# A bias read from PSUM, wider PSUM tiles for layer 0, and one shared region for tanh buffers in a two-layer attention kernel

## The chip, the cores and the metric

The kernel runs on one core of a Trainium2 chip. The metric is the device time of one execution in microseconds (us). A core has a matrix engine (TensorE, PE in the profile, with its weight loads shown apart as PEld), VectorE (DVE), ScalarE (ACT), GpSimd (POOL), and SyncE (SP), which here only issues transfers. PE writes its results to PSUM, eight banks of 512 fp32 columns on 128 partitions; the rest lies in SBUF. Everything is in fp32.

## The reference

The input `x` has 8 batches of 1024 tokens (64 x 16) with 128 features. Layer 0 is an attention of 8 heads followed by a feed-forward block; its softmax is taken twice, once over the 64 positions `m`, once over the 16 positions `g`. Layer 1 has an additive attention, a projection with batch statistics, and a recurrence over the 1024 tokens.

```python
# layer 0, per head
scores = jnp.einsum('bhlfc,bhmgc->bhlfmg', q, k) / jnp.sqrt(jnp.float32(c))
a = jax.nn.softmax(scores, axis=4)
a = jax.nn.softmax(a, axis=5)
z = jnp.einsum('bhlfmg,bhmgc->bhlfc', a, v)
# ... output projection, layer norm, relu(z1 @ w1.T + b1) @ w2.T + b2, layer norm

# layer 1: additive attention
Wi = jnp.einsum('bnd,ed->bne', B, W)
scores = jnp.einsum('d,bijd->bij', v, jnp.tanh(Wi[:, None, :, :] + Wi[:, :, None, :]))
attn = jax.nn.softmax(scores, axis=-1)
# layer 1: recurrence
yt = jax.nn.sigmoid(wx_t + yt @ Vt)
```

The largest part of the work is the tanh: for every pair of tokens i, j of a batch, 128 features. It is symmetric in i and j, so about half of the pairs are computed.

## The kernel before, in words

`fast_path` builds a list of operations with their inputs, outputs, a priority and the engines that may do each, with a cost for each engine. `Plan.emit` (L460) then walks through time: it starts whatever can start first on some engine, and among those nearly ready the one with the lowest priority number. Its order becomes the order in each engine's queue, which the chip keeps. An operation can take a buffer from a set (`Bank`), which a later operation gives back; the planner holds it until then. `port=True` on a VectorE operation tells the planner that it shares a port with GpSimd, so the two aren't planned at once. `ROWS`, `L0` and `L1` are priorities in units of batches: layer 0 of batch b+1 is planned beside layer 1 of batch b.

*Layer 0* (`layer0`, L802), for each head and 128 query tokens: `scores` (L869) are two products of 512 columns into one of two PSUM tiles `sc` of two banks. ACT takes their exponential in place (L872). VectorE sums it (L876) and inverts the sums (L877), and multiplies `sc` by them into `e` in SBUF (L880). For two query tiles together ACT takes the second exponential of `e` (L890), VectorE sums and inverts again (L893, L894), GpSimd multiplies (L904). PE transposes `e` four 128 x 128 blocks at a time (L783) into `m0` or `m1`, PSUM tiles of one bank; VectorE (in batch 0 also ACT) copies each bank to `aT` (L795, L793). `attend` (L918) multiplies with the values into `m0` or `m1`, and `gather` (L925) adds to `zs`. The projections for a head (L833, evicted in L839 or L837; L847, evicted in L795 or L793) and the hidden layer (L965, L971) go through one bank at a time as well. In the first half of batch 0 the two halves of `sa` serve as further banks (`four`). `through_bank` (L773) is the helper: a product into a bank, then an eviction.

*Layer 1* (`layer1`, L1140). For a block `it` of 128 tokens, `group` (L1006) handles 4k tokens i at a time against the tokens j from the block's start (or from the group's own start) on, in one of five SBUF slots `th` of 4 x 1024 columns (three in the first part of batch 0). The 4k rows stand in four parts c, of k rows each; within a group that doesn't begin a block, the row of part c begins at token 4 r0 + c. Either ACT does everything, one instruction for each row with the token's own column as bias (`tanh_row`, L1029); or GpSimd (`add_rows`, L1039) or VectorE write the sums and ACT takes the tanh of all that they filled in as few instructions as possible (`wide_tanh`, L1087). VectorE does a row at a time with k < 4, in a form that also writes an accumulator that nobody reads (`add_row`, L1033), and otherwise `add_rows` with both inputs in SBUF and `port` set. PE then multiplies the rows with `v` into `sa` (`times_v`, L1107), four 32-column products for the four parts side by side, and gives the slot back. When a block's rows are done, ACT takes the exponential of `sa` into `E` (L1203); there are 46 of these. The order of the blocks is set so that narrow and wide blocks share `sa`.

After the plan the recurrence runs (L1398 to L1442), as 32 chunks beside each other, and writes the output.

PSUM before: `sa` (2 banks), `sc0`, `sc1` (2 each), `m0`, `m1` (1 each).

Of the kernel before, what the change touches and what calls it, by code (L numbers as in the profile page):

```python
# [15 lines left out]
P = 128  # L16
# [395 lines left out]


class Plan:
# [45 lines left out]
    def emit(self, slack=0.15, switch=0.1, stay=0.015):  # L460
# [26 lines left out]
        def start_at(n, t, e):  # L487
            take = ops[n][5]
            if take:
                t = max(t, min(bank_free.get(c[0], 0.0) for c in take.of(e)))  # L490
# [23 lines left out]
        while any(open_.values()):  # L514
# [10 lines left out]
            if take:  # L525
                take.name, take.tile = min(take.of(e), key=lambda c: bank_free.get(c[0], 0.0))
                bank_free[take.name] = never
# [11 lines left out]
            if give:  # L539
                bank_free[give.name] = done[n] + self.LATENCY[e]  # L540
# [25 lines left out]
def fast_path(ctx: ExitStack, tc: tile.TileContext, a: dict, fits):  # L566
# [50 lines left out]
    ths = ring("th", 5, [P, 4 * N])  # L617
# [16 lines left out]
    m1 = tile_of(psum, "m1", [P, 512])  # L634
    two = (("m0", m0), ("m1", m1))
    four = two + (("sa0", sa[:, 0:512]), ("sa1", sa[:, 512:1024]))


    def early(k, name, eng):
        t = ths[k // 4][:, (k % 4) * N : (k % 4 + 1) * N].rearrange("p (h c) -> p h c", c=C)  # L640
        eng.dma_start(out=t, in_=a[name])
        return t
# [76 lines left out]
    for h in range(H):  # L719
        nc.tensor.matmul(m1[:, 0:1], wo[:, h, :], bvn[:, h : h + 1], start=h == 0, stop=h == H - 1)  # L720
    nc.vector.scalar_tensor_tensor(zb, m1[:, 0:1], float(M), bo, ALU.mult, ALU.add)
# [51 lines left out]
    def through_bank(pe, weight, r, evict, where, more, w, pri, choice=two):  # L773
# [13 lines left out]
    def copy(dst):  # L787
        def fn(e, bank):
            src = bank
            if len(dst.shape) == 3:  # L790
# [11 lines left out]
    def layer0(b):  # L802
# [16 lines left out]
        for n_part, part in enumerate(parts):  # L819
            qts = range(NT) if part is None else range(4 * part, 4 * part + 4)  # L820

            banks = four if alone and n_part == 0 else two
            for h in range(H):
# [3 lines left out]
                if alone:  # L827
                    vp, kvp = ths[3 + h // 4][:, h % 4 * N : (h % 4 + 1) * N].rearrange("p (t c) -> p t c", c=C), ("vp0", h)
                for s in range(2) if part is None else (part,):
                    cols = slice(s * 512, (s + 1) * 512)  # L830

                    def project(bank, h=h, cols=cols):
                        nc.tensor.matmul(bank, A[:, h, :], xT[:, cols], start=True, stop=True)  # L833

                    def biased(e, bank, h=h, u=u, cols=cols):
                        if e == "ACT":
                            nc.scalar.activation(u[:, cols], bank, AF.Identity, bias=ub[:, h : h + 1])  # L837
                        else:
                            nc.vector.tensor_scalar(u[:, cols], bank, ub[:, h : h + 1], None, ALU.add)  # L839

                    through_bank(project, 0.9, [kx], biased, evict(0.75), [], [("u", h % 2, s)], L0, banks)
                for s in () if alone and n_part else range(2):

                    def values(bank, h=h, s=s):
                        for i in range(4):
                            t = 4 * s + i
                            nc.tensor.matmul(  # L847
                                bank[:, i * P : (i + 1) * P], xT[:, t * P : (t + 1) * P], Wvo[:, h, :], start=True, stop=True
                            )

                    through_bank(
                        values, 0.95, [kx], copy(vp[:, 4 * s : 4 * s + 4, :]), evict(0.68), [], [kvp + (s,)], L0, banks
                    )
                for qt in qts:
                    L0 = pace(n_part, h + (qt - qts[0]) / len(qts))
                    i = (n_part * H + h) * len(qts) + qt - qts[0]
                    sc, kc = scs[i % 2], ("sc", i % 2)
# [4 lines left out]
                    r1, r2 = st[:, q, 0:G], st[:, :, G : G + M]  # L862
                    sc3 = sc.rearrange("p (m g) -> p m g", g=G)
                    e3 = e.rearrange("p (m g) -> p m g", g=G)

                    def scores(_, sc=sc, u=u, qt=qt):
                        for s in range(2):
                            cols = slice(s * 512, (s + 1) * 512)
                            nc.tensor.matmul(sc[:, cols], u[:, qt * P : (qt + 1) * P], xT[:, cols], start=True, stop=True)  # L869

                    add(("PE", 1.74), scores, r=[kx, ("u", h % 2, qt // 4)], w=[kc], pri=L0)
                    add(("ACT", 0.98), lambda _, sc=sc: nc.scalar.activation(sc, sc, AF.Exp, scale=SCALE),  # L872
                        r=[kc], w=[kc], pri=L0)

                    def first_sums(_, sc=sc, r1=r1):
                        nc.vector.tensor_reduce(r1, sc.rearrange("p (m g) -> p g m", g=G), AX.X, ALU.add)  # L876
                        nc.vector.reciprocal(r1, r1)  # L877

                    def divide(_, e3=e3, sc3=sc3, r1=r1):
                        nc.vector.tensor_tensor(e3, sc3, r1.unsqueeze(1).to_broadcast([P, M, G]), ALU.mult)  # L880

                    add(("DVE", 1.49), first_sums, r=[kc], w=[k1], pri=L0)
                    add(("DVE", 1.22), divide, r=[kc, k1], w=[ke], pri=L0)
# [15 lines left out]
                    for q in range(2):  # L899
# [7 lines left out]
                        for s in range(2):  # L907
                            through_bank(
                                transposes([e[:, t * P : (t + 1) * P] for t in range(4 * s, 4 * s + 4)]), 0.52, [ke],
# [600 lines left out]
```

## Time and profile before

| | |
|---|---|
| median of 3 runs | 5395.53 us (5393.81 to 5401.85) |
| the profiled execution | 5395.36 us, of which the span of the profile 5393.6 |
| busy in the span | PE 5044.0, PEld 2771.6, DVE 4933.6, ACT 5099.2, POOL 4496.0 us |
| tanh on ACT | 953 wide (2629 us), 2084 rows (1502 us) |
| sums for tanh | POOL 2268 (3319 us), DVE 1754 rows (1542 us) and 94 others |
| waits for a `th` slot (released by L1107) | POOL 299, DVE 40, ACT 29 us |

A group line of the profile reads: line, engine and operation, output <- inputs (tiles' names without their numbers), shape of output <- input, count; after the bar busy time in us and mean ns of one; after the second bar the engine's idle time just before these instructions and what ended it. A window line gives the length of a stretch and then, for PE, PEld, DVE, ACT and POOL, busy time and count, and at the end the granted TensorE clock and the DMA's share and rate. The ends of matmuls are modelled, so they overlap in the rows.

### The profile page before, as it was taken

The numbers are of one execution on the slowest core, as the hardware profiler recorded it, in microseconds if no ns is written. First come the engines' busy times: TensorE is split into PE (matmuls) and PEld (weight loads), VectorE is DVE, ScalarE is ACT, GpSimd is POOL, SyncE is SP. The second block draws the span as 40 slices with busy tenths as digits, with TensorE's granted clock in tenths as the row PEclk, the third lists the DMA queues.
The fourth block names the chain that finished last, engine by engine and source line by source line (L and its number), as shares of the span: only waits on it lengthen the run. The fifth ranks groups of instructions, "written<-read, shape, count | busy, mean of one in ns | idle before, by whom it ended". The sixth has DMA issues, their size and how long they took to land.

```text
span 5393.6 us, 99434 instructions
## 1 busy us (share of the span) xinstructions
PE 5044.0 (94%) x39173; PEld 2771.6 (51%) x39173; DVE 4933.6 (91%) x8326; ACT 5099.2 (95%) x4190; POOL 4496.0 (83%) x3078
## 2 busy tenths in 40 slices
PE   8999999999999999999999999999999999995566
PEld 6655554555555455555555555545555455542125
DVE  7998989899999999899998999999998999999886
ACT  5489999999999999999999999999999999999994
POOL 2364779798989899899998989898898998996992
PEclk9999999999999999999999999999999999998999
DMA  2000000000000000000000000000000000000001
GB/s 62 1 5 1 1 1 5 1 9 1 1 5 6 4 1 1 5 9 1 1 5 5 5 1 1 5 5 5 1 1 3 7 1 1 1 30 8 1 1 68
DMA packets 27341, 37.73 MB, mean 7 GB/s; under 512 B 2512, under 2 KB 19280, under 8 KB 26864
## 3 DMA queue, kind: packets, MB, share of 16 engines
q1 hardware_dynamic: 24832, 27.99, 1.6%
q8 instruction: 310, 5.08, 0.4%
q10 hardware_dynamic: 1872, 3.16, 0.2%
q14 instruction: 167, 1.37, 0.1%
q0 software_dynamic: 160, 0.13, 0.0%
HBM read 19.22 MB, written 12.06 MB: 6 GB/s over the span
## 4 chain that ended last, share of the span: by engine, by line
PE 56%; ACT 19%; DVE 18%; issue 6%; POOL 1%; DMA 0%; DVEq 0%; ACTq 0%; SPq 0%; POOLq 0%
PE sa L1107 20%; PE m L918 11%; PE sc L869 10%; ACT th L1087 10%; PE m L783 6%; ACT th L1029 5%; DVE th L1033 5%; DVE stat_e L876 2%; DVE stat_e L893 2%; DVE wx L880 2%; ACT sc L872 2%; ACT wx L890 2%; PE m L1236 2%; DVE aT L795 2%; PE m L847 1%
## 5 line engine op out<-in xcount | busy, mean ns | idle before, releaser
L1039 POOL TENSOR_TENSOR th<-wiT 128x1024 f32<-128x1024 f32 (+54 forms) x2268 | 3318.7, 1500 | 318.2 <-PE sa L1107 298.8
L1087 ACT ACTIVATE th<-th 128x4096 f32<-128x4096 f32 (+55 forms) x953 | 2629.0, 2788 | 22.6 <-DVE th L1039 9.5
L1107 PE MATMUL sa<-th,vpat 128*32 128x512 f32 (+33 forms) x24576 | 2037.4, 462 | 235.6 <-ACT th L1087 223.3
L1033 DVE TENSOR_SCALAR_CACHE_REDUCE th<-wiT 128x512 f32<-128x512 f32 (+57 forms) x1754 | 1542.3, 879 | 156.7 <-PE sa L1107 40.3
L1029 ACT ACTIVATE th<-wiT 128x384 f32<-128x384 f32 (+60 forms) x2084 | 1502.5, 792 | 29.2 <-PE sa L1107 28.9
L1107 PEld LDWEIGHTS sa<-th,vpat 128*32 128x32 f32 x24576 | 662.8, 110 | 1372.1 <-issue 844.3
L904 POOL TENSOR_TENSOR wx<-wx,stat_e 128x1024 f32<-128x1024 f32 x512 | 983.9, 1944 | 389.4 <-DVE stat_e L894 320.8
L869 PE MATMUL sc<-xT,wx 128*128 128x512 f32 x2048 | 981.2, 604 | 11.3 <-DVE wx L880 10.7
L918 PE MATMUL m<-aT,wx 128*128 128x256 f32 x3584 | 823.7, 383 | 4.7 <-DVE aT L795 4.5
L918 PEld LDWEIGHTS m<-aT,wx 128*128 128x128 f32 x3584 | 668.1, 190 | 187.5 <-issue 48.0
L880 DVE TENSOR_TENSOR wx<-sc,stat_e 128x1024 f32<-128x1024 f32 x512 | 624.2, 1219 | 25.0
L876 DVE TENSOR_REDUCE stat_e<-sc 128x16 f32<-128x1024 f32 x512 | 619.7, 1210 | 25.8 <-ACT sc L872 25.3
L795 DVE COPY aT<-m 128x512 f32<-128x512 f32 x927 | 600.3, 674 | 36.7 <-PE m L783 34.3
L783 PEld LDWEIGHTS m<-ident,wx 128*128 128x128 f32 x3940 | 443.5, 141 | 326.0 <-issue 156.9
L893 DVE TENSOR_REDUCE stat_e<-wx 128x128 f32<-128x2048 f32 x256 | 583.2, 2278 | 19.1 <-ACT wx L890 18.4
L783 PE MATMUL m<-ident,wx 128*128 128x128 f32 x3940 | 562.6, 278 | 29.7 <-DVE aT L795 14.3
L872 ACT ACTIVATE sc<-sc 128x1024 f32<-128x1024 f32 x512 | 512.7, 1007 | 62.3 <-PE sc L869 56.0
L869 PEld LDWEIGHTS sc<-xT,wx 128*128 128x128 f32 x2048 | 354.7, 190 | 374.4 <-issue 329.3
L890 ACT ACTIVATE wx<-wx 128x2048 f32<-128x2048 f32 x256 | 487.7, 1905 | 30.1 <-DVE wx L880 29.9
L894 DVE RECIPROCAL stat_e<-stat_e 128x128 f32<-128x128 f32 x256 | 243.9, 953 | 8.8
L847 PEld LDWEIGHTS m<-Wvo,xT 128*128 128x128 f32 x1080 | 134.4, 192 | 53.0 <-issue 26.9
L847 PE MATMUL m<-Wvo,xT 128*128 128x128 f32 x1080 | 145.5, 281 | 4.4 <-DVE aT L795 2.4
(183 smaller groups left out, 2887.0 us busy)
## 6 DMA issues: line engine op xcount, KB each, us to landing
xT<-in_xt_dram SPq DMA_DIRECT2D x8, 512.0 KB, 3.6
th<-in_x_dram SPq DMA_DIRECT2D x8, 512.0 KB, 6.8
parked<-X SPq DMA_DIRECT2D x16, 256.0 KB, 2.3
xr<-parked SPq DMA_DIRECT2D x8, 512.0 KB, 8.1
parked_wx<-bT SPq DMA_DIRECT2D x14, 256.0 KB, 2.0
wx<-parked_wx SPq DMA_DIRECT2D x7, 512.0 KB, 4.3
out_dram<-ot ACTq DMA_DIRECT2D x8, 256.0 KB, 2.1
out_dram<-ot SPq DMA_DIRECT2D x8, 256.0 KB, 2.8
```

The source lines that it names most:

```text
L783: nc.tensor.transpose(bank[:, i * P : (i + 1) * P], s, ident)
L795: nc.vector.tensor_copy(dst, src)
L869: nc.tensor.matmul(sc[:, cols], u[:, qt * P : (qt + 1) * P], xT[:, cols], start=True, stop=True)
L876: nc.vector.tensor_reduce(r1, sc.rearrange("p (m g) -> p g m", g=G), AX.X, ALU.add)
L880: nc.vector.tensor_tensor(e3, sc3, r1.unsqueeze(1).to_broadcast([P, M, G]), ALU.mult)
L904: nc.gpsimd.tensor_tensor(e3, e3, r2[:, q, :].unsqueeze(2).to_broadcast([P, M, G]), ALU.mult)
L918: nc.tensor.matmul(bank()[:, :256], vp[:, t, :], aT[:, t, :], start=t == 0, stop=t == NT - 1)
L1029: nc.scalar.activation(rows(c)[:, r, :], wiT[:, i0 + begin[c] :], AF.Tanh, bias=w_i(c, r))
L1033: nc.vector.tensor_scalar(rows(c)[:, r, :], wiT[:, i0 + begin[c] :], w_i(c, r), 0.0, ALU.add, ALU.add, accum_out=unused)
L1039: eng.tensor_tensor(rows(c), wiT[:, i0 + begin[c] :].unsqueeze(1).to_broadcast(shape), w_i(c).unsqueeze(2).to_broadcast(shape), ALU.add,)
L1087: nc.scalar.activation(slot()[:, a:z], slot()[:, a:z], AF.Tanh)
L1107: nc.tensor.matmul(sa[32 * c : 32 * c + 32, s:s1], vpat[:, 31 - r0 - r : 63 - r0 - r], rows(c)[:, r, s - at0 - begin[c] : s1 - at0 - begin ...
```

## The change

Four things change together; the planner then makes a new order.

1. *VectorE's bias.* `m1` goes; its bank is now `near`. For every 64 tokens VectorE copies their columns from `wiT` into a 64-column part of `near` (seven parts in turn). VectorE's additions are all `tensor_tensor` with the bias as first input, from PSUM, over `per` rows at once, and no longer set `port`. The first 64 columns of `near` take the inverted sums of layer 0 (`r1`).
2. *Layer 0 through two-bank tiles.* `sc0` and `sc1` (in the first half of batch 0 also `sa`) now serve scores, all eight transposes of a query tile, the projections and two hidden blocks at a time; single-bank products may use `m0`, `sc0` or `sc1`. The score's exponential goes from PSUM straight to `e`, and the sums and the division work on `e`.
3. *One region.* The five slots become one tile of 20 x 1024 columns. A group takes 4k (w - 4 r0) columns where there is room (`Room`, `Span`), the first part of batch 0 within the first 12 x 1024.
4. *Rectangles.* All rows of a group begin at token 4 r0. A group is filled in pieces of `per` rows, in token order; a group that ACT doesn't do by rows has one wide tanh.

```diff
+class Room:
+    def place(self, n, now, top):
+        best = None
+        for i, (a, _, _) in enumerate(self.spans):
+            t, z = now, a
+            for _, z, free in self.spans[i:]:
+                t = max(t, free)
+                if z - a >= n:
+                    break
+            if z - a >= n and a + n <= top and (best is None or (t, a) < best):
+                best = (t, a)
+        return best
...
-    ths = ring("th", 5, [P, 4 * N])
+    room = 20 * N
+    th = tile_of(work, "th", [P, room])
+    ring_room = Room(th, room)
...
-    m1 = tile_of(psum, "m1", [P, 512])
-    two = (("m0", m0), ("m1", m1))
-    four = two + (("sa0", sa[:, 0:512]), ("sa1", sa[:, 512:1024]))
+    near = tile_of(psum, "near", [P, 512])
+    two = tuple((f"sc{i}", t) for i, t in enumerate(scs))
+    three = two + (("sa", sa),)
+    any_of = (("m0", m0),) + two
...
-            banks = four if alone and n_part == 0 else two
+            wide = three if alone and n_part == 0 else two
+            banks = any_of + wide[2:]
...
-                    add(("PE", 1.74), scores, r=[kx, ("u", h % 2, qt // 4)], w=[kc], pri=L0)
-                    add(("ACT", 0.98), lambda _, sc=sc: nc.scalar.activation(sc, sc, AF.Exp, scale=SCALE),
-                        r=[kc], w=[kc], pri=L0)
+                    through_bank(
+                        scores, 1.74, [kx, ("u", h % 2, qt // 4)],
+                        lambda _, bank, e=e: nc.scalar.activation(e, bank, AF.Exp, scale=SCALE), ("ACT", 0.98), [], [ke], L0, wide,
+                    )
...
+                    def first_sums(_, e=e, s1=s1, r1=r1):
+                        nc.vector.tensor_reduce(s1, e.rearrange("p (m g) -> p g m", g=G), AX.X, ALU.add)
+                        nc.vector.reciprocal(r1, s1)
+
+                    def divide(_, e3=e3, r1=r1):
+                        nc.vector.tensor_tensor(e3, r1.unsqueeze(1).to_broadcast([P, M, G]), e3, ALU.mult)
...
-                        for s in range(2):
-                            through_bank(
-                                transposes([e[:, t * P : (t + 1) * P] for t in range(4 * s, 4 * s + 4)]), 0.52, [ke],
-                                copy(aT[:, 4 * s : 4 * s + 4, q * P : (q + 1) * P]), evict(0.68), [],
-                                [("aT", na, q, s)], L0, banks,
-                            )
+                        through_bank(
+                            transposes([e[:, t * P : (t + 1) * P] for t in range(NT)]), 1.04, [ke],
+                            copy(aT[:, :, q * P : (q + 1) * P]), evict(1.24), [], [("aT", na, q)], L0, wide,
+                        )
...
-        slot = Bank(*slots[: 3 if first_half else 5])
-
-        begin = [0 if r0 == 0 else 4 * r0 + c for c in range(4)]
...
+        slot = Span(ring_room, 4 * k * (w - 4 * r0), 12 * N if first_half else 20 * N)
+        if 4 * r0 % 64 == 0:
+            n = count.setdefault("near", 0)
+            count["near"] = n + 1
+            count["near", it] = n % 7
+            cols, own = near[:, 64 * (n % 7 + 1) : 64 * (n % 7 + 2)], wiT[:, i0 + 4 * r0 : i0 + 4 * r0 + 64]
+            add(("DVE", 0.15), lambda _, cols=cols, own=own: nc.vector.tensor_copy(cols, own), r=all_wi,
+                w=[("near", n % 7)], pri=ROWS - 0.03)
...
+        W = w - 4 * r0
+        per = (1, 1, 1, 2, 2, 4, 8, 16)[it]
+        pieces = 4 * k // per
...
-            nc.vector.tensor_scalar(
-                rows(c)[:, r, :], wiT[:, i0 + begin[c] :], w_i(c, r), 0.0, ALU.add, ALU.add, accum_out=unused
-            )
...
+            if e == "DVE":
+                own = biases[:, 4 * r0 % 64 + p * per : 4 * r0 % 64 + (p + 1) * per].unsqueeze(2).to_broadcast(shape)
+                nc.vector.tensor_tensor(rows(p), own, others, ALU.add)
+            else:
+                own = w_i(p * per, per).unsqueeze(2).to_broadcast(shape)
+                nc.gpsimd.tensor_tensor(rows(p), others, own, ALU.add)
```

In the changed kernel's numbering the lines that the prediction names are: scores L947, their exponential L951, transposes L854, copies L866 and L868, VectorE's additions L1125, GpSimd's L1128, row tanh L1118, wide tanh L1159.

More of the change, by code (lines that the diff above doesn't have):

```diff
@@ L827, in layer0 @@
                 if alone:
[L828 to L841, printed above, removed]
```

232 lines of the change are left out of this document (134 added, 98 removed).

## The prediction

> **What bounds the kernel now.** I read the page's busy lines and slices first, then the stage windows, then the rows of idle time by form. The page has four engines nearly full:
>
> ```profile
> PE 5044.0 (94%) x39173; PEld 2771.6 (51%) x39173; DVE 4933.6 (91%) x8326; ACT 5099.2 (95%) x4190; POOL 4496.0 (83%) x3078
> ...
> ACT  5489999999999999999999999999999999999994
> ```
>
> ACT has two weak slices at the start and one at the end. I cut the span at three of the 46 exponentials that read `sa` (L1203): the 1st at 421 us, the 7th at 994, the 37th at 4748 (about where layer 0 ends). Columns: length, then busy time of PE, PEld, DVE, ACT, POOL.
>
> ```profile
> 0.00:421.00 421.00, 393.31 (x1913) 260.10 (x1914) 363.16 (x486) 274.73 (x420) 181.10 (x116) 1.00 0.08 22
> 421.00:994.00 573.00, 549.40 (x3983) 311.91 (x3985) 523.33 (x783) 547.35 (x600) 440.26 (x289) 0.99 0.01 2
> 994.00:4748.00 3754.00, 3666.08 (x29061) 1998.35 (x29054) 3508.06 (x5847) 3716.94 (x2792) 3409.55 (x2346) 1.00 0.01 4
> 4748.00:5297.00 549.00, 363.25 (x3676) 135.81 (x3674) 482.16 (x1049) 532.13 (x284) 461.65 (x324) 0.94 0.03 9
> ```
>
> Before 421 us PE leads (393 of 421) and ACT idles 146 us. From 421 on ACT is the limit: idle 26, 37 and 17 us in the three later stages. PE is close behind in the long stage, idle 88 of 3754 us. So the sum to make is ACT's work by stage, with PE as the second limit.
>
> **The rows that price the edits.** Columns of a group: form, count, busy us, mean ns of one, idle before.
>
> ```profile
> L880 DVE TENSOR_TENSOR wx<-sc,stat_e 128x1024 f32<-128x1024 f32 x512 | 624.2, 1219 | 25.0
> ...
> L795 DVE COPY aT<-m 128x512 f32<-128x512 f32 x927 | 600.3, 674 | 36.7 <-PE m L783 34.3
> ...
> L1033 DVE DVE_READ_ACCUMULATOR th<-wiT 128x1 f32 x1754 | 144.7, 82 | 0.0
> ...
> L1039 DVE TENSOR_TENSOR th<-wiT 128x1024 f32<-128x1024 f32 x13 | 22.6, 1779 | 0.0
> ...
> L1033 DVE TENSOR_SCALAR_CACHE_REDUCE th<-wiT 128x1024 f32<-128x1024 f32 x7 | 8.9, 1273 | 0.2
> ...
> L872 ACT ACTIVATE sc<-sc 128x1024 f32<-128x1024 f32 x512 | 512.7, 1007 | 62.3 <-PE sc L869 56.0 <-issue 2.5 <-ACT th L1029 1.7
> ...
> L1087 ACT ACTIVATE th<-th 128x4096 f32<-128x4096 f32 x27 | 97.6, 3613 | 0.2 <-DVE th L1039 0.2
> ...
> L1087 ACT ACTIVATE th<-th 128x3072 f32<-128x3072 f32 x12 | 33.0, 2753 | 0.0
> ...
> L1203 ACT ACTIVATE E<-sa 128x1024 f32<-128x1024 f32 x26 | 26.2, 1008 | 0.0
> ```
>
> *VectorE's bias in a PSUM bank.* An addition of 1024 elements now costs 1273 + 82 ns with the accumulator's read. With both inputs in SBUF it took 1779 ns (L1039), with one in PSUM and one in SBUF 1219 ns (L880). The new one (L1125) is of the last kind: 152 ns fixed and 1.042 ns an element. The planner's order, counted in both built programs, has 1754 + 94 VectorE additions before (1.199 million elements a partition) and 1419 after (1.340 million). Before: 1542 us and some 130 for the 94. After: 1419 x 0.152 + 1.340 x 1042 = 1612, and 128 copies of 64 columns into the bank at 0.2 (26). So some 35 us less for 12% more elements. A broadcast that repeats a PSUM word is in no row: it lies between 1219 and 1779 ns for 1024; I take 1219, the row with the same memories. At 1779, 1.34 million elements x 0.55 ns add 733 us.
>
> *Two-bank tiles.* VectorE's 1075 copies of 512 (674 ns, 725 us) become 542 of 1024; 674 is 141 + 533, so one is 1207 and all 654: 71 less. Its 112 biases (82 us) become 67 of mixed width (75). With the additions VectorE loses about 114 us of 4934, which pays only where VectorE was late. ACT's 91 copies of 512 (593 ns, 54 us) become 41 of 1024 (at L872's 1007 ns, 41): 13 less. The exponential of the scores writes `e` in SBUF, not `sc`: L872 in place in PSUM has 1007 ns, L1203 from PSUM to SBUF 1008, so nothing. [...] `first_sums` reads `e` in SBUF: L876 from PSUM has 1210, L893 from SBUF 2278 for twice as much, so the same slope, and nothing.
>
> *The tanh region.* Groups take 4kW columns of 20 x 1024, not one of five slots. The mean group has 4.22 million / 1376 = 3070 columns, so some 6.6 fit for 5. That relieves POOL's 299 us, VectorE's 40 and ACT's 29 of waiting for `sa` (L1107) to free a slot. Of these only ACT's is on the path. Groups become rectangles: 11,300 elements more. ACT's wide tanh goes from 953 (2.962 million) to 1024 (3.137), its single rows from 2084 (1.262 million) to 1708 (1.098). At 0.840 ns an element (3613 - 2753 over 1024) the busy times leave 148 ns fixed for a wide one and 212 for a row. After: 1024 x 0.148 + 3137 x 0.840 = 2787; 1708 x 0.212 + 1098 x 0.840 = 1284. Together 4071 against 4132: 61 less.
>
> PE has the same products and transposes, and 1471 changes between attention rows and other products in place of 1743. A 512-column product takes 521 ns from start to start where the kind changes and 429 where not, so some 25 us come off PE.
>
> **The sum.** ACT: -61 - 13 and -1 for fewer biases against more ReLUs = -73 to -75. By stage, cutting the after program's order at the same three exponentials and pricing both alike (the prices overstate ACT by 3%, scaled to the windows): to the 1st 39 us less, to the 7th 11, to the 37th 15, to the end 4. PE does 52 us less before the 1st exponential (29 of layer 0's pairs of query tiles precede it, not 34) and gets them back before the 37th (+49, -25 for changes).
> - To the 1st: PE led with 93%; at that share it would give 56, ACT's own is 39. I take 39, the lower.
> - To the 7th: 11. PE's idle 24 covers it.
> - To the 37th: 15. PE's idle 88 falls to 88 - 15 - 49 + 25 = 49. It fits, but no more than another 49 could come here.
> - To the end 4; the recurrence (96 us) is untouched.
>
> 39 + 11 + 15 + 4 = 69. The profiled execution has 5395.4 (span 5393.6 and 1.8 around it), which is the median 5395.5 within 0.2. **Forecast 5326 us**, -1.3%.
>
> **Rivals.**
> 1. *The start gains nothing.* `e` is now held from the score's matmul on, since the matmul waits for its place (before, the division by VectorE was the first to need it). Two pairs are in flight. One pair's chain: scores, transposes, scores 1.72 + 0.87 + 1.72, exponential 1.0, sums and division 2.7, second exponential 1.9, sums 3.2, POOL 1.9, transposes 0.87 = 16 us, some 18 with hand-overs. Two in flight give 9 us a pair at best; the trace has 10.9 (16 pairs from 38 to 201 us), and VectorE has 10.5 us of work a pair to queue. At 1 us more for each of 22 pairs and no other gain at the start: 5395 - 30 (the later stages) + 22 = 5387; with the start unchanged 5365. For it: ACT's 56 us behind the score matmuls. Against: scores come right behind the transposes that free `e`, on the same engine.
> 2. *Slower: PE waits for the two-bank tiles.* `sc0` and `sc1` alone carry scores, eight transposes and the projections of layer 0. Before, scores had them to themselves and transposes had two other banks. PE issues in order: behind a blocked transpose stand the attention rows that free `th`, for which POOL, VectorE and ACT wait. It decides from 69 us / 1152 takings (512 scores, 512 transposes, 128 projections) = 0.06 us each; at 0.12 each the time is 5395 - 69 + 138 = 5464, at 0.09 5430. For it: PE in the long stage has 2% left. Against: `sc` is freed by the exponential, no longer by reduction and product, so it is held some 6 us for a score and 4 for a transpose, 20 of the 40 tile-us that two tiles have in a pair's 20 us.
> 3. *More than ACT's work.* The region and the shorter VectorE lines also take half of ACT's 80 us of idling after 421 us, or PE leads the start down to 365: 5326 - 40 = 5286, with both some 5270.
> 4. *The change doesn't free VectorE:* the PSUM broadcast runs like L1039's 1779 ns. VectorE at 4820 + 733 = 5553 becomes the bound, some 5700.
>
> **Chances.** Forecast (5300 to 5350) 48%; less at the start (5350 to 5400) 20%, of which half is faster by over 0.2% (about what a measurement here can tell from no change), 8 points within it and 2 slower; more 15%; slower by the tiles 14%, by the broadcast 3%. Faster 0.48 + 0.15 + 0.10 = 0.73; same 0.08; slower 0.19. The range leaves out the broadcast, half of the tiles' case and the lowest tail: 5275 to 5430.
>
> **What would show it.** ACT's busy time 5020 to 5030 and its rows 1708; VectorE's L1125 at 1.04 ns an element and no POOL addition longer than now; the 1st exponential of `sa` near 380 us and the 37th near 4680; PE's idle before score and transpose products near what L869 and L783 have now (11 and 39 us). If L947 or L854 wait 60 us or more for ACT or VectorE, rival 2 holds; if the 1st exponential stands at 420, rival 1. The forecast is wrong if ACT idles over 70 us more than its 294.

## The result and the profile after

The changed kernel takes 5532.1 us (median of 4 runs) where the kernel before took 5398.7 beside it: a ratio of 1.0253, 95% interval 1.0241 to 1.0266. It is slower by 133 us. The forecast was 5326, and its range ended at 5430. The profiled execution of the changed kernel spans 5530.1 us, 136.5 more than before.

The busy lines and the chain of work of the changed kernel, first of all:

```profile
PE 5046.3 (91%) x39173; PEld 2815.8 (51%) x39173; DVE 5159.8 (93%) x5689; ACT 5045.6 (91%) x3835; POOL 4469.6 (81%) x2711
...
DVE 55%; PE 26%; ACT 10%; issue 8%; POOL 1%; DMA 0%; DVEq 0%; SPq 0%; ACTq 0%; POOLq 0%
DVE stat_e L955 14%; DVE th L1125 12%; PE sa L1179 9%; DVE stat_e L972 7%; DVE wx L959 7%; ACT th L1159 6%; DVE aT L868 6%; PE sc L947 4%; PE m L995 3%; PE sc L995 3%; PE sc L854 2%; DVE stat_e L973 2%; DVE near L956 2%; ACT th L1118 2%; DVE wx L868 1%
```

ACT does 54 us less than before, as was wanted, and yet idles 484 us instead of 294. VectorE, which should have lost 114 us, does 226 more, and the chain now runs through it for 55% of the span (18% before). The largest single line of the chain is L955, the first sums. The chain of before:

```profile
PE 56%; ACT 19%; DVE 18%; issue 6%; POOL 1%; DMA 0%; DVEq 0%; ACTq 0%; SPq 0%; POOLq 0%
```

The stage windows, cut at the same three exponentials of `sa` and at the 46th (columns as before: length, then busy time of PE, PEld, DVE, ACT, POOL):

```profile
0.00:411.00 411.00, 351.39 (x1701) 233.25 (x1702) 352.75 (x382) 238.87 (x337) 166.94 (x108) 0.97 0.07 21
411.00:991.00 580.00, 549.69 (x3953) 315.34 (x3951) 559.35 (x549) 539.31 (x492) 437.36 (x266) 0.99 0.01 3
991.00:4907.00 3916.00, 3715.39 (x29306) 2064.97 (x29299) 3769.17 (x4118) 3713.92 (x2666) 3397.13 (x2044) 0.99 0.01 3
4907.00:5437.00 530.00, 358.34 (x3677) 136.66 (x3675) 421.64 (x479) 525.45 (x246) 464.68 (x290) 0.96 0.03 9
```

The long stage is 162 us longer (3754 before); the others gave 10, lost 7 and gave 19. In the long stage ACT's work is what it was (3714 against 3717), and VectorE's grew from 3508 to 3769 us, 96% of the stage.

The rows by form that answer to those shown of before:

```profile
L955 DVE TENSOR_REDUCE stat_e<-wx 128x16 f32<-128x1024 f32 x512 | 991.5, 1937 | 49.3 <-ACT wx L951 49.2
...
L951 ACT ACTIVATE wx<-sc 128x1024 f32<-128x1024 f32 x503 | 505.5, 1011 | 79.4 <-PE sc L947 66.6 <-POOL wx L983 5.5 <-POOL th L1128 4.0
...
L1159 ACT ACTIVATE th<-th 128x4096 f32<-128x4096 f32 x27 | 97.5, 3612 | 1.2 <-DVE th L1125 0.6 <-POOL th L1128 0.5
...
L1125 DVE TENSOR_TENSOR th<-near,wiT 128x1024 f32<-128x1024 f32 x26 | 31.0, 1211 | 0.0
...
L1275 ACT ACTIVATE E<-sa 128x1024 f32<-128x1024 f32 x26 | 26.2, 1009 | 0.7 <-PE sa L1179 0.7
```

Each costed row came as costed, but for the first. These are the two rows of before from which it had been costed:

```profile
L876 DVE TENSOR_REDUCE stat_e<-sc 128x16 f32<-128x1024 f32 x512 | 619.7, 1210 | 25.8 <-ACT sc L872 25.3
...
L893 DVE TENSOR_REDUCE stat_e<-wx 128x128 f32<-128x2048 f32 x256 | 583.2, 2278 | 19.1 <-ACT wx L890 18.4
```

L955 does with `e` in SBUF what L876 did with `sc` in PSUM: the same 1024 elements, read with 16 elements between one and the next. L876 had 1210 ns; L955 has 1937. The difference of 727 ns times 512 is 372 us of VectorE.

### The profile page after: what moved, and what is told of

Same layout as the page of the kernel before. It is cut to its first block, busy times and chain, and to the rows that moved or that the text cites. A ratio compares the mean times of both kernels' runs of the same rounds, so it can differ in the third digit from the quotient of the medians.

```text
span 5530.1 us, 95072 instructions
## 1 busy us (share of the span) xinstructions
PE 5046.3 (91%) x39173; PEld 2815.8 (51%) x39173; DVE 5159.8 (93%) x5689; ACT 5045.6 (91%) x3835; POOL 4469.6 (81%) x2711
## 4 chain that ended last, share of the span: by engine, by line
DVE 55%; PE 26%; ACT 10%; issue 8%; POOL 1%; DMA 0%; DVEq 0%; SPq 0%; ACTq 0%; POOLq 0%
DVE stat_e L955 14%; DVE th L1125 12%; PE sa L1179 9%; DVE stat_e L972 7%; DVE wx L959 7%; ACT th L1159 6%; DVE aT L868 6%; PE sc L947 4%; PE m L995 3%; PE sc L995 3%; PE sc L854 2%; DVE stat_e L973 2%; DVE near L956 2%; ACT th L1118 2%; DVE wx L868 1%
## 5 line engine op out<-in xcount | busy, mean ns | idle before, releaser
L1128 POOL TENSOR_TENSOR th<-wiT 128x776 f32<-128x776 f32 (+49 forms) x1901 | 3290.4, 1764 | 254.6 <-PE sa L1179 244.7
L1159 ACT ACTIVATE th<-th 128x3456 f32<-128x3456 f32 (+44 forms) x1024 | 2777.5, 2747 | 28.7 <-DVE th L1125 15.4
L1179 PE MATMUL sa<-th,vpat 128*32 128x512 f32 (+25 forms) x24576 | 2004.6, 462 | 212.9 <-ACT th L1159 197.8
L1125 DVE TENSOR_TENSOR th<-near,wiT 128x968 f32<-128x968 f32 (+45 forms) x1419 | 1545.9, 1130 | 94.2 <-PE sa L1179 88.9
L983 POOL TENSOR_TENSOR wx<-wx,stat_e 128x1024 f32<-128x1024 f32 x512 | 982.0, 1939 | 578.8 <-DVE stat_e L973 517.0
L1118 ACT ACTIVATE th<-wiT 128x440 f32<-128x440 f32 (+52 forms) x1708 | 1289.9, 820 | 23.6 <-PE sa L1179 23.5
L955 DVE TENSOR_REDUCE stat_e<-wx 128x16 f32<-128x1024 f32 x512 | 991.5, 1937 | 49.3 <-ACT wx L951 49.2
L947 PE MATMUL sc<-xT,wx 128*128 128x512 f32 x2012 | 979.2, 613 | 43.9 <-DVE aT L868 29.6
L969 ACT ACTIVATE wx<-wx 128x2048 f32<-128x2048 f32 x256 | 488.9, 1910 | 177.9 <-DVE wx L959 172.8
L959 DVE TENSOR_TENSOR wx<-near,wx 128x1024 f32<-128x1024 f32 x512 | 624.4, 1219 | 12.9
L854 PE MATMUL sc<-ident,wx 128*128 128x128 f32 x3984 | 527.2, 279 | 106.9 <-DVE aT L868 38.7
L854 PEld LDWEIGHTS sc<-ident,wx 128*128 128x128 f32 x3984 | 444.3, 143 | 300.9 <-issue 147.3
L972 DVE TENSOR_REDUCE stat_e<-wx 128x128 f32<-128x2048 f32 x256 | 582.2, 2274 | 11.0 <-ACT wx L969 11.0
L947 PEld LDWEIGHTS sc<-xT,wx 128*128 128x128 f32 x2012 | 358.5, 193 | 437.7 <-issue 328.8
L951 ACT ACTIVATE wx<-sc 128x1024 f32<-128x1024 f32 x503 | 505.5, 1011 | 79.4 <-PE sc L947 66.6
L868 DVE COPY aT<-sc 128x1024 f32<-128x1024 f32 x474 | 565.6, 1209 | 9.7 <-PE sc L854 8.8
```

What stands on the lines that cost most here:

```text
L854: nc.tensor.transpose(bank[:, i * P : (i + 1) * P], s, ident)
L947: nc.tensor.matmul(bank[:, cols], u[:, qt * P : (qt + 1) * P], xT[:, cols], start=True, stop=True)
L955: nc.vector.tensor_reduce(s1, e.rearrange("p (m g) -> p g m", g=G), AX.X, ALU.add)
L959: nc.vector.tensor_tensor(e3, r1.unsqueeze(1).to_broadcast([P, M, G]), e3, ALU.mult)
L972: nc.vector.tensor_reduce(r2, e2.rearrange("p q (m g) -> p q m g", g=G), AX.X, ALU.add)
L983: nc.gpsimd.tensor_tensor(e3, e3, r2[:, q, :].unsqueeze(2).to_broadcast([P, M, G]), ALU.mult)
```

## The experiments

**Theories.** A: the first sums read one fp32 in every 64 bytes of SBUF, and such a read is slow by itself; the rest of the change does what was forecast. B: PE waits for the two-bank tiles (rival 2), and the slow sums are incidental. C: the loss comes from a plan made with a wrong price for the sums, and goes away with the right one. D, the rival in run 4: L955 is slow because ScalarE or GpSimd use SBUF at the same time. From run 5 on the letters have the meaning that each expectation gives them. Line numbers are those of each kernel.

**1. The first sums from PSUM.** The exponential in place in the two-bank tile, which is held until the division:

```
- through_bank(scores, ..., nc.scalar.activation(e, bank, AF.Exp, scale=SCALE), ...)
+ add(("PE", 1.74), scores(held()), take=held, wait=[ke])
+ add(("ACT", 0.98), nc.scalar.activation(held(), held(), AF.Exp, scale=SCALE))
- nc.vector.tensor_reduce(s1, e.rearrange("p (m g) -> p g m", g=G), AX.X, ALU.add)
+ nc.vector.tensor_reduce(s1, held().rearrange("p (m g) -> p g m", g=G), AX.X, ALU.add)
```

> The changed kernel, but the exponential stays in place in the two-bank PSUM tile, and first_sums and the division read that tile (sums back in SBUF); the tile is given back after the division. Theory A (VectorE's first sums over a 64-byte stride in SBUF cost 1937 ns for 1210 from PSUM, 512 times = 372 us, and made VectorE the limit): the reduce is back at 1210 ns, VectorE's busy time falls from 5160 to about 4830, ACT's work by the prices of the prediction is 4054 for tanh and some 5030 in all, so with ACT's old idling of 294 the time is 5310 to 5350. Theory B (PE's waits for the two-bank tiles are the cause): the tiles are now held longer than in the changed kernel, so the time stays over 5480. Theory C (the planner's wrong cost): the planner's 1.49 us is right again, so it gives the same as A and is told apart by the other two runs.

Measured: 5395.6 us, ratio 0.9996 (0.9986 to 1.0006), the time of before. The sums have 1208 ns again, so they are cheap where they read PSUM, but no expectation is met. The exponential waits 141 us for scores, where it waits 55 in run 2; that is 86 of the 96 us that ACT idles more than there. By the edit the tile is held through the sums and the division, which fits such a wait, but the planner also made another plan, and the two were not told apart.

**2. The same sums, contiguous.** The sums then are of other elements; nothing else differs, the order of the work included:

```
- nc.vector.tensor_reduce(s1, e.rearrange("p (m g) -> p g m", g=G), AX.X, ALU.add)
+ nc.vector.tensor_reduce(s1, e.rearrange("p (g m) -> p g m", g=G), AX.X, ALU.add)
```

> The changed kernel with one edit: the first sums read e in contiguous runs of 64 instead of a stride of 16 elements. The sums are then those of other elements (the softmax is left wrong); counts, sizes, order and buffers are the same. Theory A: the reduce falls to some 1210 ns, VectorE to 4790 us, and the time to the forecast's 5326, within 5300 to 5350. Theory B: nothing about the tiles changes, so the time stays over 5480.

Measured: 5310.0 us, ratio 0.9834 (0.9817 to 0.985). In this order of work the stride alone costs 222 us, and without it the change gives 88 against the kernel before beside it, near the forecast of 69. Its busy lines, chain, and the row:

```profile
PE 4979.8 (94%) x39173; PEld 2792.2 (53%) x39173; DVE 4813.5 (91%) x5689; ACT 5019.2 (95%) x3835; POOL 4462.2 (84%) x2711
...
PE 56%; ACT 23%; DVE 13%; issue 7%; POOL 1%; DMA 0%; ACTq 0%; POOLq 0%; SPq 0%; DVEq 0%
...
L955 DVE TENSOR_REDUCE stat_e<-wx 128x16 f32<-128x1024 f32 x512 | 616.5, 1204 | 84.4 <-ACT wx L951 83.1
```

The waits show how the slow sums reached ACT, and what became of rival 2. In the changed kernel (engine, line, what it waited for, us, times, longest):

```profile
ACT wx L969 <- DVE wx L959: 172.8, 164, 7.1
...
PE sc L854 <- DVE aT L868: 41.0, 39, 3.6
...
PE sc L947 <- DVE aT L868: 29.6, 38, 2.3
```

With contiguous sums, the same tiles and the same order of work:

```profile
ACT wx L969 <- DVE wx L959: 19.0, 17, 5.1
...
PE sc L854 <- DVE aT L868: 5.0, 7, 1.5
```

ACT idles 195 us less than in the changed kernel, and 154 of them lie in one wait, that of the second exponential (L969) for VectorE's division (30 us before the change). PE's waits for the tiles were VectorE's lateness seen from PE: the copies that free the tiles stood behind slow sums. B falls.

**3. The planner told what the sums cost.** The kernel orders its work by prices. The changed kernel still carried 1.49 us for the first sums and their inverse:

```
- add(("DVE", 1.49), first_sums, r=[ke], w=[k1], pri=L0)
+ add(("DVE", 2.2), first_sums, r=[ke], w=[k1], pri=L0)
```

> The changed kernel with the planner's cost of the first sums at 2.2 us for 1.49, the computation unchanged; the planner then moves additions off VectorE (1208 for 1419) and rows back to ACT (1972 for 1708). Theory A: the 372 us stay on the chip, but are shared: tanh on ACT 4120 us for 4071, VectorE about 4930; 5380 to 5430. Theory C (the loss is a plan that doesn't fit the chip, and would go away with a right cost): under 5350. Theory B: over 5480.

Measured: 5370.8 us, ratio 0.9947 (0.993 to 0.9964), faster than before. It lies between A's range and C's: both the read and the plan count. The sums still take 1941 ns. With the price known, the planner gives VectorE 1208 additions instead of 1419 and ACT 1972 single rows instead of 1708:

```profile
PE 5006.1 (93%) x39173; PEld 2798.3 (52%) x39173; DVE 4957.6 (92%) x5475; ACT 5065.6 (94%) x4051; POOL 4520.7 (84%) x2742
...
PE 57%; ACT 20%; DVE 16%; issue 6%; POOL 1%; DMA 0%; SPq 0%; ACTq 0%; DVEq 0%; POOLq 0%
```

So of the 222 us, 161 went with a plan made for the right price, and 61 remain. A new plan can move the time by itself, so this split holds for these two plans only.

**4. The read measured alone.** Reductions and copies of 1024 fp32 appended to the kernel before, at strides of 1 to 128 elements for the reductions and 1 to 64 for the copies.

> The kernel before with a measurement appended after its output: VectorE reduces 1024 elements from SBUF and from PSUM at strides of 1 to 128 elements, and copies by VectorE and by ACT read the same at strides of 1 to 64, with no other engine at work. Theory A: from SBUF 1.2 us at stride 1 and 1.9 at stride 16, from PSUM 1.2 at both. Rival (contention with GpSimd or ACT for SBUF makes the reduce slow in the kernel): 1.2 us everywhere.

VectorE's rows by form, where 128xG is the reduction at a stride of G elements, `wx` in SBUF and `there` in PSUM:

```profile
L1452 DVE TENSOR_REDUCE total<-wx 128x4 f32<-128x1024 f32 x3 | 6.0, 1985 | 0.1
...
L1452 DVE TENSOR_REDUCE total<-wx 128x128 f32<-128x1024 f32 x3 | 5.9, 1951 | 0.0
...
L1452 DVE TENSOR_REDUCE total<-wx 128x16 f32<-128x1024 f32 x3 | 5.7, 1915 | 0.0
...
L1452 DVE TENSOR_REDUCE total<-there 128x16 f32<-128x1024 f32 x3 | 3.7, 1224 | 0.1
...
L1452 DVE TENSOR_REDUCE total<-wx 128x2 f32<-128x1024 f32 x3 | 3.6, 1213 | 0.0
L1452 DVE TENSOR_REDUCE total<-wx 128x1 f32<-128x1024 f32 x3 | 3.6, 1200 | 0.0
```

From SBUF, a stride of 2 costs next to nothing; from 4 on it costs some 700 to 800 ns, and no more at 128 than at 4. From PSUM the stride costs next to nothing (1214 ns at stride 1, 1221 to 1224 at the others). GpSimd was idle during all of the strided reductions, but the recurrence (the kernel's last part) ran between those from SBUF, so that PE and ACT were at work during most of them. The single records tell the stride from the company: the third reduction at stride 2 took 1200 ns with PE and ACT at work, the third at stride 4 took 1944 ns with no other engine at work. The copies had no other engine beside them, and ACT's pays too (1056 ns at stride 1, 2013 at 4, 1922 at 16; 1023 from PSUM at all strides); VectorE's copy goes from 693 to 1074 at stride 4 and 1025 at 16. So D falls, and the reads in run 8 say the same.

Four fp32 are 16 bytes: at a stride of 2 two of the elements read lie within 16 bytes, at 4 one, and between these strides lies the step in the rows above (1213 against 1985 ns). That two within 16 bytes are enough, however they are spaced beyond, was the author's estimate from these rows. Runs 9, 11 and 12 show it for one more pattern: pairs of neighbours with 32 elements from pair to pair took 1203 to 1204 ns.

**5 to 7. What each part of the change is worth**, against the contiguous sums' 5310 us. Five fixed slots in place of the region:

```
- slot = Span(ring_room, 4 * k * (w - 4 * r0), 12 * N if first_half else 20 * N)
+ slot = Bank(*[(f"th{i}", th[:, 4 * i * N : 4 * (i + 1) * N]) for i in range(3 if first_half else 5)])
```

> The changed kernel with the contiguous view of the first sums (sums of other elements, time alone counts; 5309.96 us in its own run), and with five slots of a fixed size for the tanh buffers in place of the one region. What is told apart: what the region is worth once the first sums cost what they did before. A (the prediction's step: of the waits for a buffer only ScalarE's 29 us lie on the path, POOL's 299 us do not): 5310 to 5340 us. B (the region brings most of the gain): above 5360 us. C (the region is worth nothing or harms): 5300 to 5312 us.

VectorE's additions as before the change:

```
- nc.vector.tensor_tensor(rows(p), own, others, ALU.add)          # own: near, in PSUM
+ nc.vector.tensor_scalar(rows()[:, j, :], ..., w_i(j), 0.0, ALU.add, ALU.add, accum_out=unused)   # per < 4
+ nc.vector.tensor_tensor(rows(p), w_i(p * per, per)..., others, ALU.add)                          # else
```

> The changed kernel with the contiguous view of the first sums (sums of other elements, time alone counts; 5309.96 us in its own run), and with VectorE's additions made as before the change: row by row with the bias as a scalar in SBUF for narrow pieces, one tensor_tensor with both operands in SBUF for wide ones, priced for the planner as before the change. What is told apart: what the bias in PSUM is worth. A (the prediction's step: ScalarE's 4132 -> 4071 us of tanh comes from VectorE's cheaper rows, and it is the larger part of the gain): 5340 to 5380 us. B (the gain comes from the transposes and the region): 5310 to 5330 us.

Transposes by four:

```
- through_bank(transposes([... for t in range(NT)]), 1.04, [ke], copy(aT[:, :, ...]), evict(1.24), ..., wide)
+ for s in range(2):
+     through_bank(transposes([... for t in range(4 * s, 4 * s + 4)]), 0.52, [ke], copy(aT[:, 4 * s : 4 * s + 4, ...]), evict(0.68), ..., banks)
```

> The changed kernel with the contiguous view of the first sums (sums of other elements, time alone counts; 5309.96 us in its own run), and with layer 0's transposes of the attention matrix four at a time through single banks, evicted in two copies of 512 in place of one of 1024. What is told apart: what the wide transposes are worth. A (the prediction's step: VectorE gives some 70 us of its fixed costs, which the planner turns into rows taken from ScalarE, shared between three engines): 5320 to 5345 us. B (no gain, since the two-bank tiles are then needed by two users and PE waits for them): 5300 to 5312 us. C (all of the gain is here): above 5360 us.

Measured: without the region 5345.0 us (35 lost; ratio to before 0.9903, 0.9887 to 0.992), without the PSUM bias 5387.9 (78; 0.9984, 0.9975 to 0.9994), without the wide transposes 5351.7 (42; 0.9919, 0.9902 to 0.9935). The bias is the largest part, and without it next to nothing is left of the gain: ACT's tanh is back at 4134 us, where it has 4087 with the contiguous sums and had 4132 before. This run still makes the 128 copies into `near` (29 us of VectorE), and the transposes by four have `m0` and the two-bank tiles, and no `m1`, so neither part stands quite as it did before the change. Each result lies 5 to 8 us beyond the upper end of A's expectation, on the side of a larger worth. The three add up to 155 us where all of it together brought 88, so they can't be read as shares: each was taken from a kernel that had the other two, and each time the planner made another plan. What the parts are worth one by one on the kernel before was not run.

**8. Writes.** As in 4, with the stride on the write side, and VectorE's reads once more:

> The kernel before, with instructions appended that stand alone: VectorE's multiplication of 1024 contiguous fp32 in SBUF by a value in PSUM, written to SBUF at strides of 1, 2, 4, 16 and 64 elements; ScalarE's copy with the same writes; and VectorE's multiplication with the same strides on the read side. A (only reads pay for the stride; writes don't): 1220 to 1240 ns for the multiplication and 1020 to 1060 for the copy at every stride of the write, and about 1930 to 2000 ns for reads at stride 4 and more. B (writes pay as reads do): some 1900 to 2000 ns from stride 4 on in both.

The timeline of this kernel where stride 2 ends and stride 4 begins (start, us, engine, line; L1451 is the multiplication, L1455 the copy):

```profile
5403.15 1.23 DVE L1451 TENSOR_TENSOR total<-there,wx 128x1024 f32<-128x1024 f32 x1 [1.18 <-ACT total L1455]
5404.41 1.11 ACT L1455 ACTIVATE total<-wx 128x1024 f32<-128x1024 f32 x1 [1.29 <-DVE total L1451]
5405.56 1.96 DVE L1451 TENSOR_TENSOR total<-there,wx 128x1024 f32<-128x1024 f32 x1 [1.18 <-ACT total L1455]
5407.55 2.01 ACT L1455 ACTIVATE total<-wx 128x1024 f32<-128x1024 f32 x1 [2.02 <-DVE total L1451]
```

Writes pay as reads do: B. The reads follow with no other engine at work. Of these four multiplications two read at a stride of 2 and two at a stride of 4; singly they took 1224, 1224, 1947 and 1957 ns:

```profile
5445.89 6.46 DVE L1460 TENSOR_TENSOR total<-there,wx 128x1024 f32<-128x1024 f32 x4
```

So the order can't be turned for nothing by an SBUF write between the exponential and the sums. The exponential's read of PSUM can turn it: ACT's copy from PSUM took 1023 ns at every stride tried.

**9 to 12. A layout that both sums read well.** The first sums add over 64 groups m of keys, the second over the 16 keys g in a group. In natural order one of them must stride by 16. If two m and two g share 16 bytes, each finds two of its elements in every 16 bytes that it reads, as at a stride of 2 (1213 ns in run 4). The four kernels below lay out `e` in this way. The core of it, as the first, third and fourth have it (the first with its own split of the keys):

```
- nc.scalar.activation(e, bank, AF.Exp, scale=SCALE)
+ nc.scalar.activation(e4, bank.rearrange("p (m i g) -> p m g i", g=G, i=2), AF.Exp, scale=SCALE)   # e4: e as p m g i
- nc.vector.tensor_reduce(s1, e.rearrange("p (m g) -> p g m", g=G), AX.X, ALU.add)
+ nc.vector.tensor_reduce(s1, e.rearrange("p (m g i) -> p g m i", g=G, i=2), AX.XY, ALU.add)
```

The first kernel pairs keys 128 apart, so its transposes take every second column of `e`:

> The changed kernel, computing the same, with the attention weights laid out in SBUF so that two keys 128 apart stand side by side: the first exponential reads PSUM in that order and writes contiguously, the first sums then read pairs (two neighbours, then 32 elements on), the second sums read every second element, and the transposes take every second column. A (what costs is one fp32 per 16 bytes, as stride 2 at 1213 and stride 4 at 1985 ns suggest, so two by line are free): the first sums 1210 to 1240 ns, the second sums in two halves of some 1210 ns each, and 5305 to 5345 us in all, below both kernels. B (any read that isn't in one line of addresses pays): the first sums some 1900 ns and the second ones 3900 for the pair, above 5500 us. C (the sums are as in A, and the price moves to the transposes' column loads or to GpSimd's division by a pattern of three dimensions, which have 143 and 1939 ns now): 5350 to 5450 us, with these rows longer.

Measured: 5367.8 us, ratio 0.9952 (0.9939 to 0.9966). Time and rows are C's: the sums have 1204 and 1216 ns, and the transposes' column loads 208 ns where they had 143. That these loads cost the 58 us against the contiguous sums is not shown: this kernel also takes the second sums of a pair in two instructions, at a price of 3.4 in place of 3.25, and the third kernel, which does so too but has its loads back at 142 ns, is only 7 us faster. The second (key 16m+8i+t at 128t+2m+i) moves the stride to the values' loads:

> The changed kernel, computing the same, with another order of the attention weights in SBUF: key 16m+8i+t lies at 128t+2m+i. The first exponential reads PSUM in that order; the first sums read every second element (m side by side in pairs), the second sums read pairs of neighbours, and the transposes take contiguous columns again; the 1120 column loads of the values take every eighth column in place of the 3992 of the transposes every second. A (in two_by_line the transposes' column loads, 208 in place of 143 ns, were what cost): these loads at 143 ns again, the sums at 1204 to 1280, the values' loads above their 194 ns, and 5305 to 5335 us. B (the loads were not the cause; the new order costs elsewhere, in the exponential or in what waits for it): 5350 to 5385 us. C (a stride of eight makes the values' loads so slow that PE waits for them): above 5385 us.

Measured: 5411.1 us, ratio 1.0022 (1.0013 to 1.003). C: the values' loads take 334 ns instead of 194 and their products 401 instead of 280, and PE's share of the chain is 70% (56% with the contiguous sums). GpSimd's division takes 2155 instead of 1939 and the first sums 1234 instead of 1204; GpSimd has 3% of the chain in all. The second sums are one instruction here, and there are as many instructions of each kind as with the contiguous sums, so these 101 us more are the order's. How they divide among the longer rows was not separated.

```profile
L928 PEld LDWEIGHTS sc<-Wvo,xT 128*128 128x128 f32 x1120 | 274.1, 334 | 23.8 <-issue 15.8
```

The third reads the values' columns from a copy of x in the new order, made once per batch by VectorE (`xTv`, in 1024 elements taken from the region):

```
+ nc.vector.tensor_copy(xTv.rearrange("p (m g i) -> p m g i", ...), xT.rearrange("p (m i g) -> p m g i", ...))
- ... xT[:, t * P : (t + 1) * P], Wvo[:, h, :], start=True, stop=True
+ ... xTv[:, t * P : (t + 1) * P], Wvo[:, h, :], start=True, stop=True
```

> The changed kernel, computing the same, with key 32m+16i+g at 32m+2g+i in SBUF (the first sums read pairs of neighbours, the second sums every second element, the transposes contiguous columns), and with one copy of x per batch in that order, from which the values' column loads read contiguously (8 copies in all; the tanh region gives 1024 elements of its 20480 for it). A (the other two orders lost to the column loads, 208 for 143 ns of the transposes in one, 334 for 194 ns of the values and 2155 for 1939 ns of GpSimd's division in the other): all three back at 143, 194 and 1939 ns, sums at 1204 to 1220, and 5310 to 5340 us, below both kernels. B (an order other than the natural one costs where it is written or waited for, not in the loads): 5350 to 5390 us.

Measured: 5361.1 us, ratio 0.993 (0.9917 to 0.9944). The loads, GpSimd's division and the sums have the durations that A said, but the time is B's. Against the contiguous sums there were two more differences, with nothing to do with the layout, both of them in the first kernel as well: the second sums of a pair came in two instructions, and were priced for it, 3.4 in place of 3.25. The fourth takes both back:

```
- for q in range(2): nc.vector.tensor_reduce(r2[:, q, :]..., e2[:, q, :]..., AX.X, ALU.add)
+ nc.vector.tensor_reduce(r2..., e2.rearrange("p q (m g i) -> p q m i g", g=G, i=2), AX.X, ALU.add)
- add(("DVE", 3.4), second_sums, ...)
+ add(("DVE", 3.25), second_sums, ...)
```

> The kernel of two_by_line_3 with its second sums in one instruction for the pair in place of two, and their price for the planner at 3.25 again in place of 3.4 (the price that sums_contiguous has); every row of two_by_line_3 had the duration it has in sums_contiguous, and yet it took 51 us longer. A (the dearer second sums, by 256 fixed costs of some 145 ns of VectorE and by the plan that the planner made from 3.4, are what was lost): 5305 to 5330 us, below both kernels. B (the new order of the keys, the copy per batch or the 1024 elements less of the tanh region are): 5345 to 5370 us.

Measured: 5315.9 us, ratio 0.9845 (0.9831 to 0.9858). Of the versions that sum the reference's groups it is the fastest. Its busy lines and the two sums:

```profile
PE 4992.7 (94%) x39173; PEld 2796.5 (53%) x39173; DVE 4804.4 (90%) x5679; ACT 5027.0 (95%) x3878; POOL 4417.3 (83%) x2689
...
L966 DVE TENSOR_REDUCE stat_e<-wx 128x16 f32<-128x1024 f32 x512 | 616.2, 1203 | 84.5 <-ACT wx L960 83.4
...
L984 DVE TENSOR_REDUCE stat_e<-wx 128x128 f32<-128x2048 f32 x256 | 584.6, 2284 | 38.2 <-ACT wx L981 36.7
```

The busy time of VectorE fell by 43 us from the third to the fourth (4846.9 to 4804.4), the time by 45. The second sums account for 19 us of VectorE's 43 (603.2 to 584.6), and for 22 the seven copies of x into the region (31.3 to 9.5; the longest took 14.3 us in the third, 2.5 in the fourth). Why the copies took longer in the third is open. How much of the time is the 256 instructions saved and how much the other plan was not separated.

## Why the prediction was wrong, step by step

- **The step that failed** is the end of the paragraph on the two-bank tiles: "`first_sums` reads `e` in SBUF: L876 from PSUM has 1210, L893 from SBUF 2278 for twice as much, so the same slope, and nothing." L876 strides, but in PSUM; L893 is in SBUF, but reads neighbours. No row of before that it cited had the two together, and the step took the pair for priced where it should have set bounds. Measured: 727 ns more, 372 us of VectorE, put at zero. The cost reached the time because VectorE had little room: 3508 us of the long stage's 3754 before (93%), 3769 of 3916 after (96%).
- **The plan's price** was not weighed for the moved sums. The prediction counted the additions in the planner's order, and did not ask whether the planner's 1.49 us still held for the moved sums. 161 of the 222 us went when the price was put right.
- *VectorE's bias*: right. L1125 has 1211 ns for 1024 where 1219 was taken; the sum of 1612 us stands against 1419 times 1130 ns, 1603 (the busy time is less, 1545.9, as records overlap). A line through its 1419 records gives 148 ns fixed and 1.040 ns an element, where 152 and 1.042 were taken. Rival 4 is out. The 1779 ns that it was built on is a mean of two kinds of records: of the 13 of L1039 on VectorE with 1024 elements, 8 had no GpSimd instruction beside them and took 1210 to 1221 ns, and 5 had one and took 2178 to 2966. Of L1125's 26 with 1024 elements, 24 ran beside GpSimd, and all took 1161 to 1224.
- *The tanh work*: right. Wide 2777.5 and rows 1289.9 make 4067 us; 4071 was forecast, with 1708 rows. The exponential from PSUM to SBUF costs 1011 ns against 1007: right.
- *VectorE's 114 us less*: right without the sums, 4813.5 against 4820. *ACT's busy time*: 5019.2 against 5020 to 5030.
- *The region*: it was said to relieve the waits for a place, of which only ACT's 29 us were held to be on the path; the sum has no term for it. The waits did not all go: with the contiguous sums ACT still waits 21 us, GpSimd 213 (299 before) and VectorE 97 (40 before). Taking the region out cost 35 us; that this is near 29 confirms nothing.
- *By stage*: read on the contiguous sums, whose stages are below, the start gave 37 us where 39 were forecast, then 20 where 11, the long stage 2 where 15, the end 22 where 4. The sum is right within 19, the split after the start is not, so that the total comes so near is in part luck. In the long stage ACT's work fell by 26 us (3717 to 3691), and the stage by 2: ACT idles 61 us there where it idled 37. What holds it up there is open. Rival 1 (the start gains nothing) is out: 384 us, and 411 even with the slow sums.

```profile
0.00:384.00 384.00, 345.55 (x1698) 231.52 (x1698) 314.19 (x381) 238.64 (x337) 165.48 (x107) 0.97 0.08 22
384.00:937.00 553.00, 543.68 (x3955) 312.74 (x3955) 514.38 (x554) 536.46 (x492) 438.23 (x266) 1.00 0.01 3
937.00:4689.00 3752.00, 3670.94 (x29301) 2049.47 (x29298) 3508.49 (x4114) 3691.25 (x2666) 3389.64 (x2044) 1.00 0.01 4
4689.00:5216.00 527.00, 347.90 (x3678) 132.50 (x3676) 419.58 (x478) 524.97 (x246) 465.38 (x290) 0.98 0.03 9
```

- *Rival 2* was given the slower side, with a sign: L947 or L854 waiting 60 us or more for ACT or VectorE. The sign came (L854 waited some 100 us for the two engines, 41 of them for the copies L868 to `aT`), and the cause was another: with contiguous sums it is some 20 us, 5 of them for these copies. A wait for a buffer names the engine that frees it, and not why that engine is late.
- *The mark that did decide*: "wrong if ACT idles over 70 us more than its 294". It idles 190 more.

## What to carry to other kernels

When an operand moves from PSUM to SBUF, look up its access pattern as well as its size: a cost is priced by a row that has the same memory and the same stride, or it is bounded. Where a planner or a hand-written order carries prices, a changed duration must be put into it, and the two effects told apart by one run with the right price. An order in which both of two reductions find two of their elements within 16 bytes made the stride's cost go away: in run 12 the first sums took 1203 ns for 1937, and the second 2284 for 2048 elements (2274 in the changed kernel). But each reader of a new order has to be looked up: in the second layout PE's column loads of the values and GpSimd's division became slower, and the kernel took 101 us more than with the contiguous sums.

## What the runs showed of the hardware

- In runs 4 and 8, at strides of 1 and 2 in SBUF, read or written, 1024 fp32 took 1200 to 1226 ns in VectorE's reductions and multiplications and 1056 to 1121 in ACT's copies (means of three); from a stride of 4 on 1866 to 2017 and 1918 to 2013. Strides of 8 to 128 cost about as much as 4. Reads of PSUM took 1214 to 1225 (VectorE, reductions and copies) and 1023 (ACT) at every stride tried.
- Pairs of neighbours, two fp32 within 16 bytes, with 32 elements from pair to pair were read at 1203 to 1204 ns for 1024 (runs 9, 11 and 12).
- PE's column loads of 128 fp32 took, in the transposes, 143 ns from neighbours (the changed kernel) and 208 at every second element (run 9), and for the values 194 from neighbours and 334 at every eighth (run 10).
- GpSimd's division by a broadcast took 2155 ns with the pattern of the second layout (the pair of neighbours shares its divisor), 1937 to 1945 with the others.
- With both inputs in SBUF (before, L1039, 1024 elements), VectorE's additions took 1210 to 1221 ns with no GpSimd instruction beside them and 2178 to 2966 with one; GpSimd's took 1886 to 1922 with no such addition of VectorE beside them, and 7322 in the one record with eight of them in a row beside it. With one input in PSUM (the changed kernel, L1125) VectorE's took 1161 to 1224 with or without GpSimd.
- PE and ACT kept the program's order: in the trace of before, PE's products form 3142 stretches of one line each and ACT's instructions 2114, in the sequence of the built program.
